# The filter products of a spectral mixer as 64x64 tensor-engine tiles, four at a time

## Chip, cores, metric

One core of one Trainium2 chip (trn2). The metric is device time in microseconds (us) of one execution, lower is better. All runs that are compared were in the fast state, and all kernels here gave correct results.

## The reference, cut to what matters

The block normalises an image batch of 8 x 128 x 128 x 96, expands it to 192 channels, and filters those in the frequency domain. The filters are three small complex tables, resized to 128 x 65 frequencies and mixed per image by softmax weights. Then come the inverse transform, a projection back, and a feed-forward net with 8-bit operands.

```python
for cw in (cw0, cw1, cw2):                       # 16x9, 8x4, 24x13, each x 192 x 2
    t = jnp.einsum('Hh,hwmc->Hwmc', Rh, cw)
    t = jnp.einsum('Ww,Hwmc->HWmc', Rw, t)       # the product that the change touches
    filts.append(jax.lax.complex(t[..., 0], t[..., 1]))
...
r = jax.nn.softmax((hmid @ fc2.T).reshape(-1, NS, MED), axis=1)
comb = jnp.einsum('shwm,bsm->bhwm', filt, r.astype(filt.dtype))
xff = xf * comb
```

## The kernel before

Three streams of work run for each image: "a" (normalise, project, transform along one axis), "s" (spectrum: transform along the other axis, filters, multiply, inverse) and "c" (last inverse step, feed-forward, output). Each action is put on a list with a planned time, the list is sorted, and the instructions are emitted in that order; every engine then keeps it. `STREAMS` gives start and length of each image's streams in plan units. So a changed number there moves instructions past one another and adds none.

A call of `filters_of` makes the filters of two pairs of frequency rows (s = 0, 1). The contraction has 52 rows, so the two values of s lie on partitions 0 and 64. Of the 192 channels of a row k, the first 128 fill a tile of 64 rows x 128 columns of the array (u = 0 for one row, u = 1 for the other); the last 64 of both rows share u = 2, each in a 64x64 tile.

```python
STREAMS = {
    "a": ((0, 118), (119.0, 243.0), (360, 335), (695, 335), ...),
    "s": ((141, 242.1), (412, 335), ..., (2087, 335), (2430, 240)),
    "c": ((465, 335), ..., (2140, 335), (2465, 240), (2705, 150)),
}
...
def filters_of(g):                                # 33 calls for each of 8 images
    pf = kept["pf"] = psz.tile([128, 2, 512], F32, name="pf", tag="pf")
    tb = kept.pop(("tb", g))
    for u, k, m0, m in ((0, 0, 0, 128), (1, 1, 0, 128), (2, 0, 128, 64), (2, 1, 128, 64)):
        for s in range(2 if g <= NG else 1):
            p = slice(64 * s, 64 * s + R)         # R = 52
            nc.tensor.matmul(
                pf[64 * k * (u == 2) : 64 * k * (u == 2) + m, s, u * 2 * L : (u + 1) * 2 * L],
                lhsT=tb[p, k * MED + m0 : k * MED + m0 + m], rhs=RW[p, :], start=True, stop=True)
...
for s in range(NS):                               # softmax weights of an image, once per image
    pl = bank("pl")[:, :MED]
    nc.tensor.matmul(pl, lhsT=hrep, rhs=fc2T[:, s * MED : (s + 1) * MED], start=True, stop=True)
```

Of the kernel before, what the change touches and what calls it, by code (L numbers as in the profile page):

```python
# [41 lines left out]
MED = 192  # L42
# [6 lines left out]
L = W // 2 + 1  # L49
# [9 lines left out]
NU = W // QW  # L59

STREAMS = {
    "a": ((0, 118), (119.0, 243.0), (360, 335), (695, 335), (1030, 335), (1365, 335), (1700, 335), (2035, 335)),
    "s": ((141, 242.1), (412, 335), (747, 335), (1082, 335), (1417, 335), (1752, 335), (2087, 335), (2430, 240)),
    "c": ((465, 335), (800, 335), (1135, 335), (1470, 335), (1805, 335), (2140, 335), (2465, 240), (2705, 150)),
}

T_WEIGHTS, T_CONST, T_ROWS = -32.0, -4.0, (10.0, 80.0)
# [205 lines left out]
def metaformer_kernel(ctx: ExitStack, tc: tile.TileContext, a: dict, out: bass.AP):  # L273
# [399 lines left out]
    def spectrum(b, t0, P):  # L673
# [46 lines left out]
        def filters_of(g):  # L720
            pf = kept["pf"] = psz.tile([128, 2, 512], F32, name="pf", tag="pf")
            tb = kept.pop(("tb", g))
            for u, k, m0, m in ((0, 0, 0, 128), (1, 1, 0, 128), (2, 0, 128, 64), (2, 1, 128, 64)):
                for s in range(2 if g <= NG else 1):
                    p = slice(64 * s, 64 * s + R)
                    nc.tensor.matmul(  # L726
                        pf[64 * k * (u == 2) : 64 * k * (u == 2) + m, s, u * 2 * L : (u + 1) * 2 * L],
                        lhsT=tb[p, k * MED + m0 : k * MED + m0 + m],
                        rhs=RW[p, :],
                        start=True,  # L730
                        stop=True,
                    )
# [110 lines left out]
        for g in range(NG + 2):  # L843
# [6 lines left out]
            if g <= NG:  # L850
                at(t + o["s_along_w_g1"] * P, along_w, g, 1)
                at(t + o["s_copy_sr"] * P + 0.2, copy_sr, g)
                at(t + o["s_along_w_g0"] * P + 0.1, along_w, g, 0)
                at(t + o["s_filters_of"] * P, filters_of, g)
                at(t + o["s_make_dmALUsubtract"] * P, make, g, "dm", ALU.subtract)
                at(t + o["s_make_dpALUadd"] * P, make, g, "dp", ALU.add)
                at(t + o["s_times_t1dm00"] * P, times, g, "t1", "dm", 0, 0)
                at(t + o["s_times_t2dp10"] * P, times, g, "t2", "dp", 1, 0)
                at(t + o["s_times_t3dm01"] * P, times, g, "t3", "dm", 0, 1)
                at(t + o["s_times_t4dp11"] * P, times, g, "t4", "dp", 1, 1)  # L860
                at(t + o["s_turn_back_g0"] * P, turn_back, g, 0)
                at(t + o["s_turn_back_g1"] * P, turn_back, g, 1)
                at(t + o["s_real_basis_g0"] * P, real_basis, g, 0)
                at(t + o["s_real_basis_g1"] * P, real_basis, g, 1)
            else:
                at(t + o["s_along_w_g0_x"] * P, along_w, g, 0)
                at(t + o["s_alone_z"] * P, alone_z, g)
                at(t + o["s_filters_of_x"] * P, filters_of, g)
                at(t + o["s_alone_t"] * P, alone_t, g)
                at(t + o["s_alone_x"] * P, alone_x, g)  # L870
# [214 lines left out]
```

## Time and profile before

| | before |
|---|---|
| time, median of 4 runs | 2888.26 us (2887.16 to 2889.86) |
| PE busy | 2737.8 us, 95% |
| ACT, DVE, POOL busy | 82%, 74%, 70% |
| one call of pf, first start to next work | 1.031 us |
| calls of pf | 264 |

PE is the matmul side of the tensor engine, PEld its weight loads, DVE, ACT and POOL the other engines. In the middle of the run PE is busy nearly always and bounds the kernel (the prediction shows the lines); the last images are different. The stretches of the last image's spectra (from its first pf call to its last) and of the tail behind it show that. In the windows view the columns are window, length, then busy us and count for each engine, the granted clock of PE, DMA share and GB/s.

```profile
2438.40:2676.10 237.70, 219.31 (x1977) 173.85 (x1976) 215.15 (x486) 187.99 (x381) 205.06 (x288) 0.99 0.58 174
2676.10:2886.40 210.30, 133.02 (x915) 77.59 (x914) 155.36 (x443) 177.32 (x328) 66.14 (x135) 0.76 0.33 106
```

In the first, PE (219 of 238) and DVE (215) are about equally full. In the second, PE is busy for 133 of 210 us, at a mean clock of 0.76: nothing taken off PE's stream before it can shorten it.

### The profile page before, as it was taken

The page shows a single profiled execution, that of the slowest core. Times are in us where ns is not written, and L with a number is a line of the kernel's source. Part 1 is how long each engine was busy: PE and PEld are TensorE (multiplying, and loading weights), DVE is VectorE, ACT ScalarE, POOL GpSimd, SP SyncE. Part 2 cuts the span into 40 slices and gives each one's busy share as a digit, 9 for nine tenths or more (in the row PEclk, how much of TensorE's full clock was granted, in tenths as well). Part 3 has the DMA queues.
Part 4 walks back from the last instruction along what each step waited for, and adds up shares of the span by engine and source line. Part 5 has one row for each costly group of instructions (what it writes and reads, how often), then busy time and mean ns, then how long its engine had stood idle before and what let it go on. Part 6 is the DMA issues. An engine that isn't in the chain of part 4 may idle for free.

```text
span 2886.4 us, 59491 instructions
## 1 busy us (share of the span) xinstructions
PE 2737.8 (95%) x20538; PEld 2121.8 (74%) x20538; DVE 2131.1 (74%) x5630; ACT 2362.5 (82%) x4972; POOL 2027.4 (70%) x3255
## 2 busy tenths in 40 slices
PE   6999999999999999999999999999999998999765
PEld 3578887787777777777777877777777876777433
DVE  3445555677877788778877788777877778899786
ACT  4775555688888889888888889888898887778887
POOL 2247775777787778777777777777777776888332
PEclk9999999999999999999999999999999999999886
DMA  5545545656565655665566655665556555665441
GB/s 167 197 159 189 163 154 182 187 189 196 166 210 185 206 181 180 195 205 191 171 200 199 199 179 186 195 206 176 193 187 200 176 181 156 189 187 153 132 132 55
DMA packets 415470, 516.21 MB, mean 179 GB/s; under 512 B 150990, under 2 KB 357718, under 8 KB 415146
## 3 DMA queue, kind: packets, MB, share of 16 engines
q1 hardware_dynamic: 415170, 512.41, 55.5%
q8 instruction: 164, 2.69, 0.4%
q14 instruction: 136, 1.11, 0.1%
HBM read 304.70 MB, written 207.64 MB: 177 GB/s over the span
## 4 chain that ended last, share of the span: by engine, by line
PE 81%; DVE 6%; ACT 6%; POOL 3%; issue 2%; DMA 2%; SPq 0%; POOLq 0%; DVEq 0%; ACTq 0%
PE px L551 15%; PE py L576 11%; PE pz L716 11%; PE pf L726 9%; PE pv L808 7%; PE pv L806 6%; PE pg L829 5%; PE ph L941 5%; PE pk L897 5%; PE pzt L538 4%; PE po L963 3%; PE pz L927 1%; ACT y L948 1%; DVE y L952 1%; ACT h L956 1%
## 5 line engine op out<-in xcount | busy, mean ns | idle before, releaser
L763 POOL TENSOR_TENSOR rr<-t,t 128x390 f32<-128x390 f32 x512 | 525.8, 1027 | 256.6 <-DVE t L756 256.4
L952 DVE TENSOR_SCALAR y<-y,b1q 128x512 f16<-128x512 f16 x768 | 413.9, 549 | 254.1 <-ACT y L948 251.6
L551 PE MATMUL px<-W1S,zT 97*128 97x240 f32 x2048 | 516.6, 374 | 8.1 <-ACT zT L541 4.9
L948 ACT CAST y<-ph 128x512 f16<-128x512 f32 x768 | 455.3, 600 | 55.4 <-PE ph L941 52.7
L922 ACT ACTIVATE z<-t,ln_m,ln_r 128x96 fp8e5<-128x96 f32 x960 | 454.9, 479 | 15.3 <-POOL ln_m L498 15.3
L551 PEld LDWEIGHTS px<-W1S,zT 97*128 97x128 f32 x2048 | 370.6, 191 | 100.0 <-ACT zT L541 23.5
L576 PE MATMUL py<-X,F 128*128 128x384 f32 x1024 | 431.1, 502 | 0.4 <-ACT X L569 0.4
L756 DVE TENSOR_TENSOR t<-dp,pf 128x390 f32<-128x390 f32 x512 | 283.9, 555 | 180.8 <-PE pf L726 143.9
L956 ACT ACTIVATE h<-y 128x1536 fp8e5<-128x1536 f16 x256 | 381.9, 1492 | 24.8 <-DVE y L952 24.7
L562 ACT ACTIVATE rl<-px 128x480 f32<-128x480 f32 x512 | 292.9, 572 | 108.3 <-PE px L551 103.1
L584 ACT COPY yst<-py 128x384 f32<-128x384 f32 x512 | 245.6, 480 | 157.4 <-PE py L576 150.4
L716 PEld LDWEIGHTS pz<-F,yt 128*128 128x128 f32 x2080 | 306.4, 191 | 90.4 <-issue 11.4
L941 PE MATMUL ph<-zT,W1q 96*128 96x512 fp8e5 x768 | 289.9, 399 | 65.3 <-DVE zT L937 48.0
L716 PE MATMUL pz<-F,yt 128*128 128x130 f32 x2080 | 322.7, 278 | 0.4 <-ACT y L948 0.4
L808 PE MATMUL pv<-w2A,xf 128*128 128x96 f32 x2080 | 303.2, 268 | 0.0
L808 PEld LDWEIGHTS pv<-w2A,xf 128*128 128x128 f32 x2080 | 300.7, 192 | 0.0
L726 PE MATMUL pf<-RW,tb 52*64 52x130 f32 (+1 forms) x4160 | 292.5, 298 | 1.5 <-POOL rr L763 1.5
L726 PEld LDWEIGHTS pf<-RW,tb 52*64 52x64 f32 (+1 forms) x4160 | 195.1, 159 | 121.2 <-issue 77.2
L699 POOL TENSOR_TENSOR tb<-tb,r 128x384 f32<-128x384 f32 (+1 forms) x264 | 280.7, 1063 | 2.5 <-DVE r L665 2.5
L756 DVE TENSOR_TENSOR t<-dm,pf 128x390 f32<-128x390 f32 x512 | 282.1, 551 | 0.0
L806 PE MATMUL pv<-w2B,xf 128*128 128x192 f32 x1040 | 266.1, 337 | 5.4 <-POOL xf L778 5.0
L981 POOL TENSOR_TENSOR t<-t,o 128x1536 f32<-128x1536 f32 x64 | 198.7, 3105 | 100.6 <-DVE o L978 100.6
(129 smaller groups left out, 5720.0 us busy)
## 6 DMA issues: line engine op xcount, KB each, us to landing
Yd<-yst SPq DMA_DIRECT2D x128, 768.0 KB
yt<-Yd SPq DMA_DIRECT2D x256, 384.0 KB
xb<-in_x SPq DMA_DIRECT2D x64, 768.0 KB
tb<-T SPq DMA_DIRECT2D x256, 192.0 KB
xr<-in_x SPq DMA_DIRECT2D x64, 768.0 KB
Vd<-gst SPq DMA_DIRECT2D x128, 384.0 KB
vin<-Vd SPq DMA_DIRECT2D x64, 768.0 KB
out<-t SPq DMA_DIRECT2D x64, 768.0 KB
```

The source lines that it names most:

```text
L551: nc.tensor.matmul(px[:, i * (MED + SCTX) : (i + 1) * (MED + SCTX)], lhsT=zTs[u % NZT][:, i0 + i, :], rhs=W1S, start=True, stop=True,)
L576: nc.tensor.matmul(py, lhsT=F1, rhs=kept["X", u][:, i0 : i0 + 2, :].rearrange("h w m -> h (w m)"), start=True, stop=True)
L716: nc.tensor.matmul(pz[:, u * 2 * L : (u + 1) * 2 * L], lhsT=y, rhs=F2[:, cs, :], start=True, stop=True)
L726: nc.tensor.matmul(pf[64 * k * (u == 2) : 64 * k * (u == 2) + m, s, u * 2 * L : (u + 1) * 2 * L], lhsT=tb[p, k * MED + m0 : k * MED + m0 + m],
L756: nc.vector.tensor_tensor(work(name), kept[d], pair(sign, c), ALU.mult)
L763: nc.gpsimd.tensor_tensor(kept["rr"][:, :, 2 * i : 2 * i + 2, :], kept[ta], kept[tb][:, :, ::-1, :], op)
L806: nc.tensor.matmul(o, lhsT=xf[:, cs, 2, :], rhs=w2B.rearrange("m n c -> m (n c)"), start=True, stop=False)
L808: nc.tensor.matmul(o[:, u * C : (u + 1) * C], lhsT=xf[:, cs, u, :], rhs=w2A, start=False, stop=(u == 1))
L922: nc.scalar.activation(z, t, AF.Identity, bias=m, scale=r, saturate=False)
L941: nc.tensor.matmul(kept["ph", n], lhsT=W1q[:, n * 128 : (n + 1) * 128], rhs=kept["zT", u], start=True, stop=True)
L948: nc.scalar.copy(kept["y", u][:, n, :], kept["ph", n])
L952: nc.vector.tensor_scalar(y, y, b1q[:, n : n + 1], 0.0, ALU.add, ALU.max)
```

## The change

The intent: all products of the filters use the same 64x64 tiling, so a call changes the tiling on entry and exit only, and four tiles run side by side throughout. Three starts of the plan move with it.

```diff
 STREAMS = {
-    "a": (... (119.0, 243.0), (360, 335), ...
+    "a": (... (119.0, 243.0), (361.0, 335), ...
-    "c": (... (2140, 335), (2465, 240), (2705, 150)),
+    "c": (... (2140, 335), (2475, 240), (2715, 150)),
...
-            for u, k, m0, m in ((0, 0, 0, 128), (1, 1, 0, 128), (2, 0, 128, 64), (2, 1, 128, 64)):
+            halves = [(u, h, u * MED + 64 * h) for u in range(2) for h in range(2)]
+            halves += [(2, k, k * MED + 128) for k in range(2)]
+            for u, h, m0 in halves:
                 for s in range(2 if g <= NG else 1):
                     p = slice(64 * s, 64 * s + R)
                     nc.tensor.matmul(
-                        pf[64 * k * (u == 2) : 64 * k * (u == 2) + m, s, u * 2 * L : (u + 1) * 2 * L],
-                        lhsT=tb[p, k * MED + m0 : k * MED + m0 + m],
+                        pf[64 * h : 64 * h + 64, s, u * 2 * L : (u + 1) * 2 * L],
+                        lhsT=tb[p, m0 : m0 + 64],
                         rhs=RW[p, :],
```

## The prediction

> **What bounds the kernel now.** First the page: busy shares, the row of PE in the slices, the chain that ended last.
>
> ```profile
> PE 2737.8 (95%) x20538; PEld 2121.8 (74%) x20538; DVE 2131.1 (74%) x5630; ACT 2362.5 (82%) x4972; POOL 2027.4 (70%) x3255
> ...
> PE   6999999999999999999999999999999998999765
> ...
> PE 81%; DVE 6%; ACT 6%; POOL 3%; issue 2%; DMA 2%; SPq 0%; POOLq 0%; DVEq 0%; ACTq 0%
> ```
>
> PE is full from the second slice on and thins out only in the last ones, and four fifths of the chain are PE. A busy PE can still hide stalls, so next the sums of one middle stretch, and what PE waited for between 450 and 2200 us.
>
> ```profile
> core 0: us, PE busy (x) PEld busy (x) DVE busy (x) ACT busy (x) POOL busy (x), PEclk, DMA share, GB/s
> ...
> 1150.00:1500.00 350.00, 348.98 (x2695) 275.29 (x2694) 272.96 (x728) 310.16 (x663) 268.73 (x433) 1.00 0.60 193
> ```
>
> ```profile
> PE pzt L538 <- ACT V L818: 3.5, 5, 0.7
> PE ph L941 <- DVE zT L937: 1.6, 5, 0.3
> PE px L551 <- ACT zT L541: 0.9, 1, 0.9
> ```
>
> PE is busy for 349 of 350 us at full clock, and in 1750 us it waited 6.0 us for other engines. So there every nanosecond taken off PE's in-order stream should come off the time, until the next engine binds: ACT, at 310 of 350 us. Most of ACT's idle time is spent waiting for PE (in the waits of ACT in this stretch yst on py has 110.9 us, y on ph 33.5, rl on px 31.7), so it would move along.
>
> The change touches one product, pf at L726. Its groups with shapes apart:
>
> ```profile
> L726 PE MATMUL pf<-RW,tb 52*128 52x130 f32 x2080 | 191.2, 299 | 1.5 <-POOL rr L763 1.5
> L726 PE MATMUL pf<-RW,tb 52*64 52x130 f32 x2080 | 119.9, 298 | 0.0
> L726 PEld LDWEIGHTS pf<-RW,tb 52*128 52x128 f32 x2080 | 140.2, 187 | 88.7 <-issue 76.7 <-DMA yt<-Yd 2.6 <-POOL rr L763 2.0
> ```
>
> Each float32 product runs as two passes, so 2080 products give 4160 records, 16 in a full call (8 in the one call per image that uses half of the rows). There are 33 calls for each of 8 images, 264 in all. The means (298 ns) overlap each other and price nothing; the starts do. The timeline of PE, asked for in ever narrower windows around one call, gives these rows (one from each of four windows):
>
> ```profile
> 1506.82 1.10 PE L726 MATMUL pf<-RW,tb 52*128 52x130 f32 x16
> ```
>
> ```profile
> 1507.03 0.50 PE L726 MATMUL pf<-RW,tb 52*128 52x130 f32 x6
> ```
>
> ```profile
> 1507.46 0.45 PE L726 MATMUL pf<-RW,tb 52*64 52x130 f32 x8
> ```
>
> ```profile
> 1507.85 0.60 PE L941 MATMUL ph<-zT,W1q 96*128 96x512 fp8e5 x2
> ```
>
> The call starts at 1506.816, its 64-column part at 1507.462, the next work at 1507.847: 1.031 us, in two parts of 646 and 385 ns. I worked out the same interval for every call from the starts in the trace: of 255 full calls that stand alone the middle 80% lie at 1.029 to 1.032 us, and the 8 half calls take 1.01. The starts within the call:
> - 128-column part, two row tiles side by side: rounds start at 0, 215, 326 and 438 ns, and the next part at 646. A round streams 111 ns; the first is 104 longer, as it waits for its weights; the last is 97 longer, as the array empties before the next part.
> - 64-column part, four tiles side by side (their starts are 6 to 7 ns apart): rounds at 0 and 162, next work 223 after that. The weights cost 51 ns, the emptying 112.
>
> **What the Trainium skill says.** "TensorEngine Tiling (Array Packing)", Key Properties: changing the tiling mode, not just the tile, drains the engine, and tiles load and multiply in parallel. The trace agrees: 97 and 112 ns beyond a round at the two ends, and overlapped starts. "TensorE: Matmul & The Clock Gate", LDWEIGHTS: a load takes columns / 1.2 ns, 107 for 128 columns and 53 for 64; the two exposed loads, 104 and 51, agree. The same page ("Wait — 56ns, not 53.3ns?") puts the least distance of two matmul starts at about 25 ns; here tiles start 6 to 7 ns apart, so for different tiles the trace decides. [...]in this call four loads stand by 1506.93, two of them for the same tiles whose first passes run from 1506.82 to 1507.03, so a second set of weights loads behind the first even in one row group.
>
> **The change part by part.**
> - Streaming, unchanged. Before: two rounds of products of 128 columns and one of 64, each of two passes, 6 rounds. After: 12 products of 64 columns, four at a time, 3 rounds of two passes, 6 again: 666 ns both ways. Splitting the wide products wins no arithmetic.
> - Removed: the change from 64x128 tiles to 64x64 inside the call. That takes away one emptying (97) and one exposed load (51).
> - Made shorter: the first exposed load is 64 columns instead of 128, 104 becomes 51, 53 less.
> - Kept: entry from the full array and the way back.
> - Sum after: 162 + 4 x 111 + 223 = 829 ns, against 1031. So 202 ns a call, x 264 = 53.3 us.
> - Added: 1040 products, so 2080 more MATMUL and LDWEIGHTS records each, 48 instructions a call instead of 32. In a call that PE started live after a wait (2443.98 us), the second tile's first load came 36 ns after the first tile's, with that tile's four instructions to issue between, some 9 ns each; 48 x 9 = 432 ns, below 829, so by this estimate issuing does not bind.
> - Moved: two streams start 1 or 10 units later in the plan. The order listing shows that tiling alone leaves every engine's order as it was; the plan's shifts put other instructions at 1815 of PE's 16263 places, all in the stretches of 5 to 20% and 85 to 95% of its order. No work is added. Such shifts look like a fit to the shorter calls; I credit them with 3 us and take 10 either way for their doubt.
>
> **What reaches the end.** The records of L726 in four stretches, divided by 16, give 172 calls in 450:2200, 32 in 190:450, 26 in 2200:2450 and 31 in 2450:2680 (sum 261 for 4160/16 = 260, by rounding). PE is busy there for 99.7, about 98, 97 and about 90%. At 202 ns and estimated shares that reach the end of 95, 85, 80 and 50%: 33.0 + 5.5 + 4.2 + 3.1 = 46 us. With 3 for the plan, 49: 2888 - 49 = 2839; I say 2838. What is lost: ACT goes from 310 of 350 to 310 of 342.5 us (90.5%), so more short waits of PE for ACT and for banks. After 2680 us there is no pf, so the last 207 us gain nothing.
>
> **Rivals.**
> 1. ACT, or its banks, takes the bound over. For: 88.6% busy in the middle, and in-order queues lock together. Against: its idle time is mostly waiting for PE, and PE waited only 6 us. If half the gain were lost: about 2861.
> 2. Four tiles do not load behind each other's streaming. The only 64x64 stretch so far is two rounds long, so loading weights for a third was never seen there. For: twice the loads per microsecond. Against: second-pass loads start while the first streams, and the 128-column part loaded its third and fourth rounds unseen. If each new product exposed its 51 ns load, two a call: 27 us less gain, about 2865.
> 3. The plan's shift does more than the tiling. For: the last 430 us have most of PE's holes, where order matters. Against: no work goes away. Good, it gives 10 more, 2828; bad, 2850.
> 4. The drain into a 64x64 tiling costs more than into 64x128: nothing in the trace shows that; 50 ns would cost 13 us, about 2851.
>
> **Range and chances.** All 53 us and a small help from the plan give 2830 or a little below; 2% is 2830.4. Full gain and a good plan together are needed to pass it: 0.17. Rivals 1, 2 and 4 or a bad plan lead to 2850 to 2865, still within 2%. A slowdown by 58 us needs a mechanism that nothing shows: 0.01. Range 2824 to 2857.
>
> **What would show it right or wrong.** Right: starts of a call at 0, 162, then every 111 ns, next work at about 829; one form of pf, 52*64, x6240; PE's busy time in the middle stretches still above 99%; ACT near 90% there. Calls at 950 or more with rounds of 160 mean rival 2; a longer gap ahead of the call, rival 4; calls at 829 with new PE waits for ACT, rival 1; a gain or loss outside 190 to 2450 us, rival 3.

## The result, and the profile after

The changed kernel takes 2852.83 us (median of 4, 2849.47 to 2855.48) against 2888.26: 35 us less. The ratio of the fast runs is 0.9876, 95% interval 0.9859 to 0.9893. Ratios here are the mean time of one kernel's fast runs over that of the other's of the same rounds, so not quite the ratio of the medians that are quoted. The predicted 2838 was 15 us too low, and inside its range.

The page of the changed kernel, the same lines as before:

```profile
PE 2696.3 (94%) x22618; PEld 2109.1 (74%) x22618; DVE 2130.0 (75%) x5630; ACT 2358.3 (83%) x4972; POOL 2024.5 (71%) x3255
...
PE   6999999999999999999999999999999998988765
...
PE 78%; DVE 9%; ACT 6%; POOL 3%; issue 2%; DMA 1%; SPq 0%; POOLq 0%; DVEq 0%; ACTq 0%
```

PE executes 2080 more passes (x22618 against x20538) and is busy for 41 us less. The groups with shapes apart now have one form of pf (columns as in the prediction's rows: busy us, mean ns, idle before):

```profile
L729 PE MATMUL pf<-RW,tb 52*64 52x130 f32 x6240 | 239.8, 282 | 1.7 <-POOL rr L766 1.7
```

```profile
L729 PEld LDWEIGHTS pf<-RW,tb 52*64 52x64 f32 x6240 | 174.3, 134 | 88.3 <-issue 77.3 <-POOL rr L766 2.8 <-DMA yt<-Yd 2.0
```

The time before a call's first load ("issue", 77.3 us) is what it was (76.7): entering a call costs the same. The timeline of PE around one call:

```profile
1502.05 0.90 PE L729 MATMUL pf<-RW,tb 52*64 52x130 f32 x24
1502.88 0.59 PE L576 MATMUL py<-X,F 128*128 128x384 f32 x1
```

The next work starts 0.83 us after the call. Of 256 full calls the middle 80% lie at 0.826 to 0.829 us (predicted 0.829), with rounds of four at 0, 162, 273, 383, 494 and 605 ns. So the call itself became what was predicted, and the middle of the run took it nearly whole:

```profile
1150.00:1500.00 350.00, 348.59 (x3030) 277.73 (x3029) 280.88 (x739) 315.10 (x678) 275.02 (x430) 1.00 0.60 194
```

PE is still busy for 348.6 of 350 us, ACT for 90.0% of it. One image in the steady middle (first pf call to the next image's first) takes 325.9 instead of 332.2 us: 6.3 us less, of 33 x 0.203 = 6.7 that its calls lost.

Most of what is missing is at the end. The last image's spectra and the tail of the changed kernel:

```profile
2398.50:2637.00 238.50, 215.84 (x2200) 172.43 (x2199) 208.88 (x477) 182.92 (x370) 203.08 (x288) 0.97 0.56 172
2637.00:2853.70 216.70, 139.48 (x953) 82.83 (x952) 158.31 (x452) 182.93 (x340) 67.66 (x134) 0.74 0.32 104
```

The spectra of the last image gained nothing (238.5 against 237.7), and the tail became 6.4 us longer.

### The profile page after: what moved, and what is told of

Same layout as the page of the kernel before. It is cut to its first block, busy times and chain, and to the rows that moved or that the text cites. A ratio compares the mean times of both kernels' runs of the same rounds, so it can differ in the third digit from the quotient of the medians.

```text
span 2853.7 us, 63672 instructions
## 1 busy us (share of the span) xinstructions
PE 2696.3 (94%) x22618; PEld 2109.1 (74%) x22618; DVE 2130.0 (75%) x5630; ACT 2358.3 (83%) x4972; POOL 2024.5 (71%) x3255
## 4 chain that ended last, share of the span: by engine, by line
PE 78%; DVE 9%; ACT 6%; POOL 3%; issue 2%; DMA 1%; SPq 0%; POOLq 0%; DVEq 0%; ACTq 0%
PE px L551 15%; PE py L576 11%; PE pz L716 10%; PE pv L811 7%; PE pf L729 7%; PE pv L809 6%; PE pg L832 5%; PE ph L944 5%; PE pk L900 4%; PE pzt L538 4%; PE po L966 3%; DVE y L955 2%; DVE t L759 2%; ACT y L951 2%; ACT h L959 2%
## 5 line engine op out<-in xcount | busy, mean ns | idle before, releaser
L766 POOL TENSOR_TENSOR rr<-t,t 128x390 f32<-128x390 f32 x512 | 519.8, 1015 | 234.5 <-DVE t L759 234.4
L699 POOL TENSOR_TENSOR tb<-tb,r 128x384 f32<-128x384 f32 (+1 forms) x264 | 286.6, 1085 | 2.5 <-DVE r L665 2.5
L779 POOL TENSOR_TENSOR xf<-rr 128x390 f32<-128x390 f32 x256 | 232.2, 907 | 15.8
L729 PE MATMUL pf<-RW,tb 52*64 52x130 f32 x6240 | 239.8, 282 | 1.7 <-POOL rr L766 1.7
```

The costliest lines, as they stand in the source:

```text
L729: nc.tensor.matmul(pf[64 * h : 64 * h + 64, s, u * 2 * L : (u + 1) * 2 * L], lhsT=tb[p, m0 : m0 + 64], rhs=RW[p, :], start=True, stop=True,)
L766: nc.gpsimd.tensor_tensor(kept["rr"][:, :, 2 * i : 2 * i + 2, :], kept[ta], kept[tb][:, :, ::-1, :], op)
```

## The experiments

### 1 to 4: the tiles and the plan apart

All combinations of the two parts, and the two shifts of the plan apart. The edits, against the changed kernel:

```diff
e1_tiles_only:         plan of the kernel before (360; 2465 and 2705), 64x64 tiles
e2_plan_only:          plan of the changed kernel, tiles of the kernel before
e3_tiles_first_shift:  -(2475, 240), (2715, 150)   +(2465, 240), (2705, 150)
e4_tiles_last_shift:   -(361.0, 335)               +(360, 335)
```

> The 64x64 tiles with the plan of the kernel before: every engine's order as before. The calls of pf measured 826 ns in the changed kernel, so PE's stream is 53 us shorter here too. Theory A (the 15 us that did not arrive were lost to the shifts of the plan, above all the 10 units of the last two streams, which push work into the tail): 2838 to 2846 us. Theory B (the stretch of the last image and the tail are set by other engines, and the shifts do nothing or help): 2852 to 2860 us.

> The tiles of the kernel before with the plan of the changed one. Theory A: slower than before, 2894 to 2900 us. Theory B: 2884 to 2890 us, no different from before or a few us faster.

> Changed kernel with the shift by 10 of the last two output streams taken back; the shift by 1 of the third input stream stays. Theory A: 2840 to 2847 us, most of the missing time back. Theory B: 2853 us or more.

> Changed kernel with the shift by 1 of the third input stream taken back; the shift by 10 of the last two output streams stays. Between the first and second batch of spectra the changed kernel gained 3.2 us where the steady batches gain 6.3. If the shift by 1 costs this, the run is 3 us faster than the changed kernel, about 2850; if it helps, slower than 2853.

| kernel | median us | fast-run ratio to before (95%) |
|---|---|---|
| tiles only | 2843.26 | 0.9843 (0.9830 to 0.9857) |
| plan only | 2896.26 | 1.0032 (1.0023 to 1.0042) |
| tiles, first shift | 2847.68 | 0.9857 (0.9844 to 0.9871) |
| tiles, last shift | 2850.36 | 0.9862 (0.9849 to 0.9876) |
| before, same rounds | 2887.53 | |

Theory A holds (experiment 3 lies 0.7 us above its range). The tiles alone give 44 us, the plan alone costs 9, and each shift costs on top of the tiles: the first 4.4 us, the last 7.1, by the medians. The interval of the tiles alone lies clear of the changed kernel's, but overlaps those of the single shifts, so these two costs rest on the traces that follow.

**Why the last shift costs.** The tail of the tiles alone, in the same two windows:

```profile
2392.70:2630.30 237.60, 214.80 (x2232) 172.65 (x2231) 215.93 (x486) 186.76 (x381) 204.78 (x288) 0.98 0.58 174
2630.30:2840.10 209.80, 131.23 (x920) 76.23 (x918) 155.20 (x443) 176.94 (x329) 66.10 (x135) 0.78 0.32 106
```

I counted in each trace the units of the feed-forward net's second products (po, at L963 or L966, 256 in all) that start after the last pf call: 43 before and with the tiles alone, 45 in the three kernels with the last shift. Tails in that order: 210.3 and 209.8, against 216.7 (changed), 215.6 (plan only) and 216.6 us (tiles with the last shift). The shift by 10 puts two units of output work behind the last spectra, so a tail unit costs about (216.7 - 209.8) / 2 = 3.4 us.

The upper window shows a second thing: with the tiles alone too, the last image's spectra take 237.6 us as before, though PE is busy for 4.5 us less. What its calls saved became waiting. These are PE's two largest waits in that window, before and with the tiles alone:

```profile
PE ph L941 <- DVE zT L937: 11.3, 8, 4.0
PE pv L806 <- POOL xf L778: 4.2, 6, 1.5
```

```profile
PE ph L944 <- DVE zT L940: 12.9, 11, 4.0
PE pv L809 <- POOL xf L781: 5.6, 6, 2.1
```

All its waits there rose from 18.0 to 22.3 us. DVE, at 216 of 238, is now the fullest engine, but that its work sets the length is not shown: in the changed kernel it has 7 us less to do there (208.9), and the stretch is no shorter (238.5).

**Why the first shift costs.** What PE waited for from 420 to 800 us, with the tiles alone (columns: us in total, times, longest; hrep is what the softmax weights are made of):

```profile
PE pl L644 <- DVE hrep L638: 2.0, 1, 2.0
```

and in the changed kernel:

```profile
PE pl L644 <- DVE hrep L638: 4.0, 2, 2.2
```

This product (pl) makes the softmax weights; PE must stand still for the small chain of DVE before it, for one image more than before. Standing still costs more than the wait, as the windows of the tiles-only kernel around it show:

```profile
421.00:424.70 3.70, 3.70 (x26) 2.74 (x24) 2.84 (x8) 1.69 (x4) 3.34 (x5) 1.00 0.19 53
424.70:428.20 3.50, 1.54 (x9) 1.07 (x8) 2.82 (x3) 1.42 (x4) 2.08 (x3) 1.00 0.37 154
428.20:431.60 3.40, 3.40 (x23) 2.79 (x25) 0.72 (x3) 0.48 (x1) 0.00 (x0) 0.50 0.21 77
```

PE waits for 1.96 us between 424.95 and 426.91, and from 428.2 its clock is granted at half. By the clock records that lasts 10.2 us with the tiles alone and in the kernel before, and 13.7 us in the changed kernel and with the first shift. Half of the 3.5 us more is 1.7 us. Between 450 and 800 us PE is busy for 344.75 us with the first shift and 347.80 with the tiles alone: 3.1 us less, 1.7 of them the second wait. Together that is 4.8 of the 5.7 us between the two traced runs. But the kernel of experiment 7 has the same order up to there as the tiles alone and also had 13.7, so a part of the difference is chance.

The kernel of experiment 5 shows where chance comes in. It makes the same wait, and no half clock follows:

```profile
437.74 0.59 PE L644 MATMUL pl<-fc2T,hrep 36*128 36x192 f32 x2 [1.95 <-DVE hrep L638]
```

```profile
433.24:436.65 3.41, 2.55 (x17) 1.69 (x16) 2.67 (x4) 2.48 (x7) 3.41 (x5) 1.00 0.00 0
436.65:440.06 3.41, 2.32 (x16) 2.00 (x16) 1.86 (x3) 0.31 (x1) 0.95 (x2) 1.00 0.57 231
```

In the clock records of each trace all changes of the clock lie whole multiples of 3.413 us apart (to 5 ns). In the eight traces in which half clock followed this wait, of 1.96 to 2.23 us, the wait falls into one such step (in one it runs 0.06 us over), of which PE is busy for only 1.2 to 1.5 us. In experiment 5 the wait is split between two steps. That fits a clock judged step by step, but it is one trace; no run set where the steps fall.

### 5: one more change of tiling in a call

```diff
-for u, k, m0, m in ((0, 0, 0, 128), (1, 1, 0, 128), (2, 0, 128, 64), (2, 1, 128, 64)):
+for u, k, m0, m in ((0, 0, 0, 128), (2, 0, 128, 64), (2, 1, 128, 64), (1, 1, 0, 128)):
```

> Kernel before with the same products in another order: 128 columns, then the four of 64 columns, then 128 columns again, so that each call changes the tiling twice more inside instead of once. If the gain of the change is the emptying and the exposed load of a tiling change, a call takes 215 + 208 + 162 + 215 to 223 + 215 + 223 = about 1.24 us against 1.03, 210 ns more; x 264 = 55 us of PE's stream, and with the share of 44 of 53 that arrived from the tiles alone the time is about 2933 us (2925 to 2945). If the gain came from narrower products or from anything other than the changes of tiling, the order of the products does nothing: 2885 to 2890.

Measured: 2933.07 us, ratio 1.0156 (1.0139 to 1.0173) to 2887.89 of its rounds. The timeline of one call:

```profile
1505.54 1.30 PE L726 MATMUL pf<-RW,tb 52*128 52x130 f32 x16
```

In another call of this run I read rounds at 0, 215, 423, 585, 806 and 1021 ns and the next work at 1229. Each entry to a tiling exposes a load (104 ns for 128 columns, 51 for 64), each exit an emptying (97 to 112). A call now has two changes of tiling inside instead of one, and the added one takes 1229 - 1029 = 200 ns (a load of 104 and an emptying). The same products in another order cost 45 us: a tiling change inside the call costs what was priced. The change saves one, 148 of the about 202 ns that a call loses; some 53 come from the narrower products, whose first load exposes 51 instead of 104 ns.

### 6: one column of tiles after the other

```diff
-            for u, h, m0 in halves:
+            for u, h, m0 in sorted(halves, key=lambda p: p[1]):
```

> Changed kernel with the twelve products of a call sorted so that the three of the left columns (with both row halves) come first, then the three of the right columns: the same tiles and work, but only two different tiles side by side in the order. If tiles work in parallel whatever the order (each with its own queue), the call stays at 826 ns and the time at 2853. If products start strictly in order, there are twelve rounds of two instead of six of four: 162 + 11 x 111 + 112 = about 1495 ns a call, 670 more, and at 264 calls and a share of 0.83 to 0.94 some 3000 to 3020 us.

Measured: 2909.42 us, ratio 1.0073 (1.0058 to 1.0089), and one call in the timeline:

```profile
1507.61 1.17 PE L729 MATMUL pf<-RW,tb 52*64 52x130 f32 x24
1508.71 0.60 PE L944 MATMUL ph<-zT,W1q 96*128 96x512 fp8e5 x2
```

Neither expectation: the call takes 1.10 us, between 0.83 and 1.50. The starts come in pairs that read as two series, each spaced like a call of its own: 0, 162, 272, 383, 494, 605 ns and 285, 447, 558, 669, 780, 891 ns. The records do not name the tile; if the second series is the right column, it starts before the left column's last three rounds, which stand before it in the program, and is left alone at the end. On that reading products of other tiles are taken ahead of their turn, but only so far. In any case "four at a time" depends on the order in which the products are issued. With this order the same tiles are slower than the wide ones before (1.10 us a call against 1.03).

### 7: the last output streams earlier

```diff
-(2465, 240), (2705, 150)     # plan of the kernel before, with 64x64 tiles
+(2465, 225), (2700, 150)
```

> 64x64 tiles with the plan of the kernel before, but the last two output streams moved the other way: the one of image 6 gets 225 instead of 240 plan units, and that of image 7 starts at 2700 instead of 2705. After the last pf call the shift by 10 left 45 of 256 units of second products instead of 43, and the tail was 216.7 instead of 209.8 us. Theory A (units left for the tail cost about 3.4 us each): about 41 left, 2835 to 2840 us, a version better than all so far. Rival (the stretch of the last spectra is full on DVE and POOL, and pressing more output work into it delays it by as much): 2841 to 2850 us.

Measured: 2845.78 us, ratio 0.9849 (0.9833 to 0.9864): the rival. The tail shrank to 205.5 us with 42 units left, but the last image's spectra grew from 237.6 to 244.8 us:

```profile
2396.30:2641.10 244.80, 217.26 (x2263) 174.02 (x2262) 220.91 (x504) 196.15 (x398) 207.83 (x301) 0.99 0.58 174
```

DVE did 5 us more work there. Pressing output work into this stretch is paid for in it: 7.2 us, against 4.3 gained in the tail.

### 8 to 12: the third input stream earlier

```diff
-(360, 335)                   # plan of the kernel before, with 64x64 tiles
+(359, 335)                   # then 358, 356, 353; 359 once more
```

> 64x64 tiles with the plan of the kernel before, but the third input stream starts at 359 instead of 360. The shift to 361 cost about 4 us (2847.7 with it, 2843.3 without). If this is a matter of one input stream overlapping the next image's start, going the other way gains 1 to 4 us, 2839 to 2842; if 360 is a local best that any reordering spoils, 2844 to 2850.

> 64x64 tiles, plan of the kernel before, third input stream at 358. In the traces so far PE's clock is granted at half from about 428 us on for 10.2 us (tiles only) or 13.7 us (changed kernel, tiles with the shift to 361), and with the start at 359 not at all there. Theory A (an earlier third input stream fills the thin stretch at the end of the first image's spectra, so the half-clock stretch stays away, worth about 5 us): no half clock near 428 us, 2836 to 2842 us. Rival (that stretch came and went by chance): it is back in this run, 2841 to 2848 us.

> The same with the third input stream at 356. Theory A: as at 358, no half clock near 428 us, 2834 to 2842 us. Rival: 2841 to 2848 us with the half-clock stretch back.

> The same with the third input stream at 353. Theory A: no half clock near 428 us, 2832 to 2842 us, unless the earlier input holds back the first image's spectra, then up to 2848. Rival: 2841 to 2848 us with the half-clock stretch back.

> The best version so far (64x64 tiles, third input stream at 359, all else as in the plan before) once more, to tell a real gain over the tiles alone (2843.3) from chance. If the gain is real: 2836 to 2841.5 us and again no stretch of half clock near 428 us. If it was chance: 2842 to 2846 us, or the half clock is back.

| start | median us | ratio (95%) | half clock between 400 and 800 us |
|---|---|---|---|
| 360 (tiles only) | 2843.26 | 0.9843 (0.9830 to 0.9857) | 10.2 us at 428 |
| 359 | 2839.39 | 0.9827 (0.9811 to 0.9843) | none |
| 359 again | 2840.99 | 0.9836 (0.9822 to 0.9849) | none |
| 358 | 2842.15 | 0.9847 (0.9833 to 0.9860) | none |
| 356 | 2845.22 | 0.9862 (0.9846 to 0.9877) | 10.2 us at 716 |
| 353 | 2861.88 | 0.9908 (0.9892 to 0.9924) | 6.8 at 442, 10.2 at 721, 10.2 at 742 |

At 359 PE's long wait for hrep is gone, and with it the half clock, in both runs. This is the window from 410 to 450 us, first of the tiles alone, then of the first run at 359:

```profile
410.00:450.00 40.00, 37.77 (x255) 29.37 (x254) 24.18 (x57) 19.75 (x40) 19.70 (x28) 0.87 0.33 111
```

```profile
410.00:450.00 40.00, 36.73 (x267) 28.03 (x265) 26.77 (x73) 25.05 (x52) 21.30 (x34) 1.00 0.40 139
```

PE looks less busy at 359 and does more: 267 matmuls instead of 255, since at half clock the same work takes longer. Theory A of experiments 9 to 11 holds for the first image (no half clock near 428 us at 358, 356 and 359; at 353 there is some at 442), and its times do not follow (2861.88 at 353 lies above every expectation): at 358 PE waits 5.3 us for the new image's input instead, and at 356 and 353 the half clock appears one image later. Both runs at 359 have medians below the tiles alone, by 2 to 4 us, and experiment 12 meets its own test of a real gain, but the intervals overlap. By stage both gain 4.1 us more than the tiles alone in image 0 and give back 1.2 in image 1 and 2.4 to 2.8 in image 6. What is shown is a version that beats both kernels, at 2839 to 2841 us; that it beats the tiles alone is not.

## Why the prediction was right, and where it was not

Gains in us by stage, from the starts of the first pf call of each image in the traces (before minus the kernel named). The predicted column is the prediction's sum over nearly the same stretches; sums are of unrounded numbers.

| stage | predicted for the tiles | tiles only | changed kernel |
|---|---|---|---|
| up to the first call | 0 | 1.2 | 2.3 |
| image 0 | 5.5 | 6.5 | 4.8 |
| images 1 to 5 | 33.0 | 32.0 | 28.2 |
| image 6 | 4.2 | 5.9 | 4.5 |
| image 7 | 3.1 | 0.1 | -0.8 |
| tail | 0 | 0.5 | -6.4 |
| sum | 46 | 46.3 | 32.7 |

- **The call** was right: 0.826 us against 0.829. That the tiling change saved is its larger part (148 of 202 ns) is shown by experiment 5, which adds one and costs 45 us; the rest, the shorter first load, is read from the starts (215 ns to the second round before, 162 after).
- **The share that reaches the end** was right in sum (46.3 in the traced run, 44 by medians). By stage the last image was wrong: half of its gain was credited and none came, because PE waited there instead, mostly for DVE and POOL (4.3 us more in all). Images 0 and 6 came 1 to 2 us above their estimates; for image 0 the prediction had read PE as about 98% busy, where the record has 258.02 of 260 us, 99%. The 1 to 2 us up to the first call are no gain of the change, since the order there is the same in all kernels. That these errors cancel in the sum is luck.
- **The plan's shift** is the step that failed: "I credit them with 3 us". It was taken for "a fit to the shorter calls"; it costs 9 to 10 (2852.8 against 2843.3 with the tiles, 2896.3 against 2887.5 without). The listing of the order (not among the recorded runs; by the traces, PE's matmuls change places from 428 to 738 us and from 2466 to 2690 us) had said that it moves work in two stretches, and that no work goes away; from that no sign follows. I took the sign from a guess at the author's purpose. Rival 3 had the right size (10 either way). Its place was half right: of the 13.6 us between the last two columns, 7.8 lie in the last image and the tail, as it expected, and 3.8 in images 1 to 5, nearly all of it in image 1 (3.3 gained against 6.5).
- **Rival 1** is true in a small way: PE's waits for other engines between 450 and 2200 us rose from 6.0 to 10.8 us, of which 1.7 is the wait for hrep that the first shift adds. **Rivals 2 and 4** are false: rounds stay 111 ns apart, and the time before the first load of a call is the same.
- What stays open: how much of the first shift's 4 us is the wait that it adds and how much is the chance length of the half clock; what sets the length of the last image's spectra; and why the second series of experiment 6 starts at 285 ns.

## What to carry to other kernels

Price a change on a full in-order engine by the starts of its instructions, not by their busy time, and give it only where that engine is the one waited for: here the middle kept 94% of it and the last image none. Small products that share a tiling belong together, ordered so that neighbours use different tiles; here each tiling change inside a call cost 150 to 200 ns, more than a round of work (111 ns). When a plan or schedule is moved along with a change, measure the two apart: the tiles alone were better than the whole change.

## What the Trainium skill lacked or had wrong

- "TensorEngine Tiling (Array Packing)", Key Properties, says that changing the mode drains the engine and gives no cost. Here one change cost 97 to 112 ns of emptying plus an exposed load of 51 ns (64 columns) or 104 ns (128 columns), with float32 operands in two passes.
- The same page does not say that the order of issue matters. The same twelve products took 0.826 us with the four tiles in turn and 1.098 us with one column of tiles first.
- "TensorE: Matmul & The Clock Gate" (HAM oscillation) puts the rule at no idle gaps over some 3.4 us. Here one wait of 1.96 us, in a stretch of 3.5 us where PE was busy for 1.54, was followed by 10.2 us of half clock. Waits of 1.96 to 2.23 us at that place were followed by 10.2 or 13.7 us of it in eight traces, and a wait of 1.95 us by none in one (experiment 5).
